# A Macaron block with an SSM and FP4 layers on one core: one projection for B, C and dt, other engines for part of the layernorm, and a new order with tables of its own at the ends

## The chip, the core and the metric

The kernel runs on one core of a Trainium2 chip. The metric is the device time of one execution in microseconds (us); the figure given for a kernel is the median of its runs. The engines are PE (TensorE), DVE (VectorE), ACT (ScalarE), POOL (GpSimd) and SP (SyncE, which issues the transfers). Each works through its own instructions in the order in which they were written; semaphores order them across engines.

## What is computed

The input `x` is 32 batches of 512 rows by 256 columns, in float32. Each batch goes through three layers, each with a layernorm in front and a residual sum behind:

```python
x = x + 0.5 * ffn(layernorm(x))      # "ffn 0"
x = x + ssm(layernorm(x))            # "ssm"
x = x + 0.5 * ffn(layernorm(x))      # "ffn 1"

def ffn(x):                          # w_gate, w_up: 704 x 256, w_down: 256 x 704
    xq = fp4(x)                      # per 16 values: scale = max|x| / 6, round to the FP4 grid
    h = silu(xq @ fp4(w_gate).T) * (xq @ fp4(w_up).T)
    return fp4(h) @ fp4(w_down).T

def ssm(x):                          # 16 states per column
    Bm, Cm = split(x @ W_in + b_in)  # 16 + 16 columns
    dt = clip(softplus((x @ W_dt1 + b_dt1) @ W_dt2 + b_dt2), 1e-7, 1e6)
    a = exp(A * dt)
    b = expm1(A * dt) / (A * dt) * dt * Bm * x
    h[l] = a[l] * h[l - 1] + b[l]    # a scan over the 512 rows, for each column and state
    return sum(h * Cm, states) + D * x
```

## The kernel before

**Layout.** A batch of 512 rows lies in SBUF as four tiles of 128 rows (`x0` to `x3`, one per stage). The FFN works per row tile: `gate` and `up` (L676), `silu` and `up copy` on ACT, `product` on POOL (L699, for the first tile of ffn 0 on DVE, L692), then the quantizing of the hidden 704 columns, six transposes (L710), and `down` (L722) with the residual (L726); `sum` (L729) copies the result from PSUM. The SSM works on transposed data, columns on partitions, 512 rows along the free axis: `bc` and `dt1` are two products with `xT` (L741), each with a bias step on ACT (L745, L752); `dt2` (L757), softplus (L761) in place in PSUM, and a clip on DVE (L764) give `dt`. B and C go through DRAM (`rows`) and come back broadcast to all partitions (L780, L782). For each half of the columns and each pair of states: exp and tanh on ACT (L789, L792), `x b` on POOL (L796), `e`, `e x b` and the scan on DVE (L803, L806, L809), `h c` on POOL (L812), and PE adds the states up in PSUM (L818). expm1 is made from tanh, since expm1(t) = (exp(t) + 1) tanh(t / 2).

**Layernorm** (L502). For each of four row tiles DVE computes bn_stats and their aggregation; POOL makes the reciprocal root and the shift of all four in four instructions on four columns each (L512 to L519); ACT applies them (`normal`, L522).

**Quantizing** (L527). DVE takes the maximum of each block, scales, inverts and makes the quotient (L544 to L550). The maximum and the reciprocal lie in PSUM. ACT squares the quotient and applies a line to it (`square` L554, `curve` L556, both to bfloat16); PE adds that number to the quotient in PSUM and takes it away again (`grid`, L563), whereby the quotient is rounded to the grid; ACT copies it out (`rounded`, L569) and POOL multiplies it by the scale (`value`, L570).

**Order.** Nothing is scheduled by the framework. `Plan` gets every step with the buffers it reads and writes. Each has a time from the table `WHEN`, plus `PERIOD` (3379) times the number of its batch; `Plan.run` takes the steps by that time, each as soon as all that it depends on has been taken and its buffers are free, and writes them out in that order. So the steps of several batches interleave on each engine, and the same order repeats from batch to batch. The weights are quantized in the same plan, at the start.

Of the kernel before, what the change touches and what calls it, by code (L numbers as in the profile page):

```python
# [16 lines left out]
P = 128  # L17
# [13 lines left out]
WHEN = {  # L31
        "weights load": (7249, 7248, 7249, 7249, 6726, 6726, 6642, 6642, 6642, 6841, 6841, 6841,
        6841),
        "weights x top": (7249, 7065, 7353),
        "weights x scale": (7250, 7248, 7385),
        "weights x rinv": (7250, 7248, 7391),
        "weights x quotient": (7250, 7248, 7391),
        "weights x square": (7250, 7249, 7392),
        "weights x curve": (7250, 7249, 7392),
        "weights x grid": (7250, 7249, 7557),  # L40
        "weights x rounded": (7250, 7249, 7557),
        "weights x value": (7250, 7249, 7558),
        "weights turn": (7251, 7251, 7249, 7249, 7558, 7558),
        "weights turned": (7251, 7251, 7250, 7251, 7558, 7558),
        "weights load down": (7065, 6579),
        "weights h top": (7558, 6642),
        "weights h scale": (7571, 6642),
        "weights h rinv": (7571, 6642),
        "weights h quotient": (7571, 6643),
        "weights h square": (7590, 6643),  # L50
        "weights h curve": (7590, 6643),
        "weights h grid": (7590, 6643),
        "weights h rounded": (7590, 6643),
        "weights h value": (7795, 7065),
        "weights turn down": (7795, 7795, 7699, 7661),
        "weights turned down": (7897, 7814, 8179, 7699),
        "weights zero rows": (8077, 8345),
        "in load": (0,),
        "ffn 0 stats": (1267, 1773, 601, 2361),
        "ffn 0 mean": (1913, 2355, 1536, 3584),  # L60
        "ffn 0 var + eps": (4038,),
        "ffn 0 rstd": (4045,),
        "ffn 0 - mean": (3609,),
        "ffn 0 shift": (4249,),
        "ffn 0 normal": (4499, 5056, 6579, 4467),
        "ffn 0 x top": (6643,),
        "ffn 0 x scale": (6726,),
        "ffn 0 x rinv": (6822,),
        "ffn 0 x quotient": (6835,),
        "ffn 0 x square": (6841,),  # L70
        "ffn 0 x curve": (6873,),
        "ffn 0 x grid": (6880,),
        "ffn 0 x rounded": (6950,),
        "ffn 0 x value": (6969,),
        "ffn 0 xqT turn": (7065, 7129),
        "ffn 0 xqT turned": (7136, 7168),
        "ffn 0 tile 0 gate": (7353, 7251),
        "ffn 0 tile 0 silu": (7437, 7321),
        "ffn 0 tile 0 up": (7577, 7558),
        "ffn 0 tile 0 up silu": (7584, 7571),  # L80
        "ffn 0 tile 0 h top": (7590,),
        "ffn 0 tile 0 h scale": (7609,),
        "ffn 0 tile 0 h rinv": (7661,),
        "ffn 0 tile 0 h quotient": (7705,),
        "ffn 0 tile 0 h square": (7737,),
        "ffn 0 tile 0 h curve": (7808,),
        "ffn 0 tile 0 h grid": (7814,),
        "ffn 0 tile 0 h rounded": (7897,),
        "ffn 0 tile 0 h value": (8045,),
        "ffn 0 tile 0 turn h": (8301, 8192),  # L90
        "ffn 0 tile 0 turned h": (8352, 8339),
        "ffn 0 tile 0 down": (8397,),
        "ffn 0 tile 0 sum": (8461,),
        "ffn 0 tile 1 gate": (7385, 7392),
        "ffn 0 tile 1 silu": (7449, 7507),
        "ffn 0 tile 1 up": (7622, 7667),
        "ffn 0 tile 1 up copy": (7718, 7699),
        "ffn 0 tile 1 product": (7795,),
        "ffn 0 tile 1 h top": (7923,),
        "ffn 0 tile 1 h scale": (8000,),  # L100
        "ffn 0 tile 1 h rinv": (8032,),
        "ffn 0 tile 1 h quotient": (8121,),
        "ffn 0 tile 1 h square": (8179,),
        "ffn 0 tile 1 h curve": (8205,),
        "ffn 0 tile 1 h grid": (8217,),
        "ffn 0 tile 1 h rounded": (8275,),
        "ffn 0 tile 1 h value": (8416,),
        "ffn 0 tile 1 turn h": (8493, 8441),
        "ffn 0 tile 1 turned h": (8544, 8512),
        "ffn 0 tile 1 down": (8563,),  # L110
        "ffn 0 tile 1 sum": (8781,),
        "ffn 0 tile 2 gate": (8083, 8064),
        "ffn 0 tile 2 silu": (8096, 8070),
        "ffn 0 tile 2 up": (8134, 8345),
        "ffn 0 tile 2 up copy": (8256, 8390),
        "ffn 0 tile 2 product": (8429,),
        "ffn 0 tile 2 h top": (8576,),
        "ffn 0 tile 2 h scale": (8653,),
        "ffn 0 tile 2 h rinv": (8704,),
        "ffn 0 tile 2 h quotient": (8729,),  # L120
        "ffn 0 tile 2 h square": (8813,),
        "ffn 0 tile 2 h curve": (8838,),
        "ffn 0 tile 2 h grid": (8857,),
        "ffn 0 tile 2 h rounded": (8953,),
        "ffn 0 tile 2 h value": (8979,),
        "ffn 0 tile 2 turn h": (9088, 9081),
        "ffn 0 tile 2 turned h": (9165, 9126),
        "ffn 0 tile 2 down": (9222,),
        "ffn 0 tile 2 sum": (9267,),
        "ffn 0 tile 3 gate": (8077, 8109),  # L130
        "ffn 0 tile 3 silu": (8089, 8211),
        "ffn 0 tile 3 up": (8928, 8985),
        "ffn 0 tile 3 up copy": (9069, 9094),
        "ffn 0 tile 3 product": (9101,),
        "ffn 0 tile 3 h top": (9357,),
        "ffn 0 tile 3 h scale": (9376,),
        "ffn 0 tile 3 h rinv": (9440,),
        "ffn 0 tile 3 h quotient": (9472,),
        "ffn 0 tile 3 h square": (9510,),
        "ffn 0 tile 3 h curve": (9529,),  # L140
        "ffn 0 tile 3 h grid": (9587,),
        "ffn 0 tile 3 h rounded": (9613,),
        "ffn 0 tile 3 h value": (9677,),
        "ffn 0 tile 3 turn h": (9837, 9843),
        "ffn 0 tile 3 turned h": (9869, 9856),
        "ffn 0 tile 3 down": (9920,),
        "ffn 0 tile 3 sum": (9984,),
        "ssm stats": (8768, 8992, 9517, 10048),
        "ssm mean": (9325, 9369, 9933, 10093),
        "ssm var + eps": (10099,),  # L150
        "ssm rstd": (10150,),
        "ssm - mean": (10157,),
        "ssm shift": (10163,),
        "ssm normal": (10182, 10169, 10227, 10176),
        "ssm xT turn": (10233, 10246),
        "ssm xT turned": (10304, 10310),
        "ssm bc": (10425,),
        "ssm bc bias": (10489,),
        "ssm rows": (10656,),
        "ssm dt1": (10317,),  # L160
        "ssm dt1 bias": (10451,),
        "ssm dt2": (10464, 10521),
        "ssm softplus": (10598, 10617),
        "ssm dt": (10681, 10688),
        "ssm skip": (11481, 13229),
        "ssm load b": (10720, 10790, 10854, 11270, 11232, 11712, 11648, 11917, 12115, 12294,
        12563, 12723, 13005, 13139, 13318, 13792),
        "ssm load c": (10809, 11161, 11328, 11846, 11641, 11974, 12153, 12345, 12627, 12825,
        13190, 13101, 13568, 13945, 14029, 14041),
        "ssm exp": (10925, 11021, 11059, 11014, 11289, 11341, 11347, 11027, 11750, 11993, 12038,  # L170
        12000, 12006, 11961, 12422, 12352, 12582, 12179, 12569, 12813, 12934, 12941, 13088, 13113,
        13376, 13120, 13382, 13305, 13753, 13849, 13504, 13811),
        "ssm tanh": (10976, 11033, 11110, 11283, 11334, 11494, 11737, 11693, 11878, 11987, 12077,
        12102, 12281, 12262, 12486, 12403, 12614, 12710, 12845, 12774, 13043, 13069, 13273, 13254,
        13491, 13408, 13670, 13734, 13837, 13907, 14093, 14125),
        "ssm x b": (10726, 11155, 11206, 11661, 11616, 12064, 11897, 12288, 12537, 12633, 12883,
        13017, 13209, 13574, 13657, 13971),
        "ssm e": (10982, 11104, 11129, 11296, 11507, 11520, 11763, 11699, 11885, 12025, 12134,
        12141, 12377, 12339, 12512, 12435, 12678, 12742, 12915, 12857, 13049, 13081, 13344, 13261,
        13587, 13523, 13715, 13773, 13920, 13933, 14163, 14214),  # L180
        "ssm e x b": (10995, 11136, 11213, 11373, 11577, 11603, 11827, 11801, 11936, 12057, 12243,
# [99 lines left out]
        "ffn 1 tile 3 down": (18112,),  # L281
        "ffn 1 tile 3 sum": (18157,),
        "out store": (19712,),
}


class Buf:
# [599 lines left out]
```

## Time and profile before

| | before |
|---|---|
| median of 3 runs | 3604.15 us (3602.44 to 3604.26) |
| the profiled execution | 3604.13 us |
| its span, first to last instruction | 3602.2 us |
| granted TensorE clock, mean | 0.984 |
| busy: PE, DVE, ACT, POOL | 3348.0, 3409.9, 3385.7, 3332.3 us |
| idle DVE time between 480 and 3360 us | 17.8 us of 2880 |
| ACT table loads | 284, 1283 ns each |

A group of instructions is one line of the profile: the line of the kernel, the engine, the operation, the tile written and the tiles read (buffer numbers left out), the shapes and the count; then the busy time of the group in us and the mean of one instruction in ns; then the time in which the engine sat idle just before them, and whose end it waited for. TensorE runs a float32 product as two matmul records. A wait is told as the engine and the line that waited, what ended the wait, the sum in us, how many there were, and the longest. A line of the table by stages names the stretch and its length, then each engine's busy time and number of instructions, then the granted TensorE clock, the busy share of the DMA engines, and GB/s. In the list of instructions by time each line has the start, the duration, and how many equal ones it merges.

### The profile page before, as it was taken

The page shows a single profiled execution, that of the slowest core. Times are in us where ns is not written, and L with a number is a line of the kernel's source. Part 1 is how long each engine was busy: PE and PEld are TensorE (multiplying, and loading weights), DVE is VectorE, ACT ScalarE, POOL GpSimd, SP SyncE. Part 2 cuts the span into 40 slices and gives each one's busy share as a digit, 9 for nine tenths or more (in the row PEclk, how much of TensorE's full clock was granted, in tenths as well). Part 3 has the DMA queues.
Part 4 walks back from the last instruction along what each step waited for, and adds up shares of the span by engine and source line. Part 5 has one row for each costly group of instructions (what it writes and reads, how often), then busy time and mean ns, then how long its engine had stood idle before and what let it go on. Part 6 is the DMA issues. An engine that isn't in the chain of part 4 may idle for free. (4 is left out here: it accounts for less than half of the span.)

```text
span 3602.2 us, 51333 instructions
## 1 busy us (share of the span) xinstructions
PE 3348.0 (93%) x16604; PEld 2443.6 (68%) x16826; DVE 3409.9 (95%) x5280; ACT 3385.7 (94%) x5813; POOL 3332.3 (93%) x1963
## 2 busy tenths in 40 slices
PE   5779999999999999999999999999999999999966
PEld 3457777667767767777766776776777776777654
DVE  3699999999999999999999999999999999999992
ACT  4689999999999999999999999999999999999973
POOL 2589999999999999999999999999999999999992
PEclk9899999999999999999999999999999999999988
DMA  1354545444545545454544454444555454445440
GB/s 45 112 173 166 173 164 176 165 169 165 176 171 170 165 158 175 170 173 164 177 165 169 165 176 170 170 165 159 176 171 173 163 177 165 168 161 169 171 170 12
DMA packets 186652, 578.36 MB, mean 161 GB/s; under 512 B 19664, under 2 KB 54032, under 8 KB 186384
## 3 DMA queue, kind: packets, MB, share of 16 engines
q1 hardware_dynamic: 184816, 574.89, 46.7%
q8 instruction: 133, 2.18, 0.2%
q14 instruction: 135, 1.11, 0.1%
q10 hardware_dynamic: 1568, 0.18, 0.0%
HBM read 556.12 MB, written 18.87 MB: 160 GB/s over the span
## 5 line engine op out<-in xcount | busy, mean ns | idle before, releaser
L676 PE MATMUL pt<-w_guT,xqT 128*128 128x352 f32 x4096 | 1317.4, 466 | 26.1 <-DVE dt L764 16.3
L812 POOL TENSOR_TENSOR hs<-hs,bc 128x1024 f32<-128x1024 f32 x512 | 1214.0, 2371 | 9.3 <-DVE hs L809 2.6
L809 DVE TENSOR_TENSOR_SCAN hs<-ab,eb 128x512 f32<-128x512 f32 x1024 | 1202.4, 1197 | 4.5
L796 POOL TENSOR_TENSOR bx<-xT,bc 128x1024 f32<-128x1024 f32 x512 | 1171.2, 2294 | 30.3 <-DVE eb L806 15.9
L676 PEld LDWEIGHTS pt<-w_guT,xqT 128*128 128x128 f32 x4096 | 753.3, 192 | 409.7 <-DVE dt L764 24.0
L792 ACT ACTIVATE eb<-dt,a_half 128x512 f32<-128x512 f32 x1024 | 708.1, 700 | 36.1 <-DVE hs L809 29.5
L806 DVE SCALAR_TENSOR_TENSOR eb<-eb,a_inv,bx 128x512 f32<-128x512 f32 x1024 | 734.9, 743 | 2.7
L722 PE MATMUL pt<-w_dT,hqT 128*128 128x256 f32 x3072 | 717.0, 383 | 14.8 <-ACT hqT L715 14.8
L789 ACT ACTIVATE ab<-dt,a_sb 128x512 f32<-128x512 f32 x1024 | 700.8, 727 | 1.5
L803 DVE SCALAR_TENSOR_TENSOR eb<-ab,eb 128x512 f32<-128x512 f32 x1024 | 684.5, 682 | 11.4 <-ACT eb L792 7.6
L722 PEld LDWEIGHTS pt<-w_dT,hqT 128*128 128x128 f32 x3072 | 580.1, 192 | 140.4 <-ACT hqT L715 32.9
L818 PE MATMUL py<-ident,hs 128*128 128x128 f32 x4096 | 536.1, 276 | 26.1 <-POOL hs L812 25.8
L818 PEld LDWEIGHTS py<-ident,hs 128*128 128x128 f32 x4096 | 469.4, 142 | 102.0 <-POOL hs L812 38.3
L570 POOL TENSOR_TENSOR h_q<-h_q,h_sc 128x704 f32<-128x704 f32 x258 | 360.3, 1397 | 53.2 <-ACT h_q L569 52.6
L699 POOL TENSOR_TENSOR h<-h,sl 128x704 f32<-128x704 f32 x224 | 379.0, 1692 | 27.4 <-ACT h L696 22.4
L544 DVE TENSOR_REDUCE q<-h 128x44 f32<-128x704 f32 x258 | 227.0, 880 | 68.6 <-POOL h L699 43.8
L710 PE MATMUL pt<-ident,h_q 128*128 128x128 f32 x1536 | 237.0, 278 | 41.2 <-ACT h L696 24.1
L563 PE MATMUL q<-h_m,eye 128*128 128x192 bf16 (+1 forms) x873 | 191.6, 305 | 70.9 <-ACT h_m L556 62.0
L710 PEld LDWEIGHTS pt<-ident,h_q 128*128 128x128 f32 x1536 | 180.5, 141 | 110.3 <-ACT h L696 51.8
L563 PEld LDWEIGHTS <-eye 128*128 128x128 bf16 x1300 | 125.2, 99 | 183.9 <-issue 106.8
L715 ACT COPY hqT<-pt 128x256 f32<-128x256 f32 (+1 forms) x512 | 233.9, 487 | 6.1 <-PE pt L710 5.7
L686 ACT ACTIVATE sl<-pt 128x352 f32<-128x352 f32 x512 | 222.5, 463 | 16.6 <-PE pt L676 13.8
(78 smaller groups left out, 4134.6 us busy)
## 6 DMA issues: line engine op xcount, KB each, us to landing
bc<-rows SPq DMA_DIRECT2D x1024, 512.0 KB, 4.1
x<-in_L_attn_x_dram SPq DMA_DIRECT2D x32, 512.0 KB, 5.2
out_dram<-x SPq DMA_DIRECT2D x32, 512.0 KB, 7.3
rows<-bc SPq DMA_DIRECT2D x32, 64.0 KB, 3.4
xn<-in_L_ffn_w_up_dram SPq DMA_DIRECT2D x6, 128.0 KB, 2.2
h<-in_L_ffn_w_down_dram SPq DMA_DIRECT2D x2, 352.0 KB, 3.4
xn<-in_L_ffn_w_gate_dram SPq DMA_DIRECT2D x5, 128.0 KB, 2.2
w_dt_sb<-in_L_attn_W_dt_dram ACTq DMA_DIRECT2D x2, 64.0 KB, 5.5
```

Of the source, the lines that this page charges most:

```text
L676: pe.matmul(to()[:, :HALF], lhsT=xqT()[:, c, j * P : (j + 1) * P], rhs=w_guT()[:, c, o : o + HALF], start=(c == 0), stop=(c == NC - 1),)
L699: op("POOL", "product", lambda sl=sl, h=h: g.tensor_tensor(h(), h(), sl(), ALU.mult), [h, sl], [h])
L710: pe.transpose(pt()[:, i * P : (i + 1) * P], hq()[:, kcol[k] : kcol[k] + P], ident)
L722: pe.matmul(po()[:, :DM], lhsT=hqT()[:, k, :], rhs=w_dT()[:, k, :], start=(k == 0), stop=False,)
L789: op("ACT", "exp", lambda c=c, i=i, k=k, ab=ab: s.activation(ab()[:, i, :], dt()[:, c, :], AF.Exp, scale=a_sb[:, c, k : k + 1]), [(dt, c)] ...
L792: op("ACT", "tanh", lambda c=c, i=i, k=k, eb=eb: s.activation(eb[i](), dt()[:, c, :], AF.Tanh, scale=a_half[:, c, k : k + 1]), [(dt, c)], ...
L796: op("POOL", "x b", lambda c=c, bx=bx, bn=bn: g.tensor_tensor(bx().rearrange("p n l -> p l n"), xT()[:, c, :].unsqueeze(2).to_broadcast([P ...
L803: op("DVE", "e", lambda i=i, ab=ab, eb=eb: v.scalar_tensor_tensor(eb[i](), ab()[:, i, :], 1.0, eb[i](), ALU.add, ALU.mult), [(ab, i), eb[i ...
L806: op("DVE", "e x b", lambda c=c, i=i, k=n + i, eb=eb, bx=bx: v.scalar_tensor_tensor(eb[i](), eb[i](), a_inv[:, c, k : k + 1], bx()[:, i, : ...
L809: op("DVE", "scan", lambda i=i, h=h, ab=ab, eb=eb: v.tensor_tensor_scan(h()[:, i, :], ab()[:, i, :], eb[i](), 0.0, ALU.mult, ALU.add), [(a ...
L812: op("POOL", "h c", lambda h=h, cn=cn: g.tensor_tensor(flat(h()), flat(h()), flat(cn()), ALU.mult), [h, cn], [h])
L818: pe.matmul(py()[:, j, :], lhsT=h()[:, i, j * P : (j + 1) * P], rhs=ident, is_transpose=True, start=False, stop=False, skip_group_check=True,)
```

## The change

- `bc` and `dt1` become one product with 96 output rows and one bias step (`project`): dt1's 64 rows first, B's and C's 32 behind.
- The layernorm of the SSM gets its sums from ACT: `sum` of ffn 0 also gives the sum of each row, DVE makes the negative mean of it (`mean`), and ACT squares the difference and sums that (`spread`, four). POOL applies the layernorm (`normal`, four).
- In all three layernorms, var + eps and the shift are one DVE instruction each; POOL keeps the power (`rstd`).
- The `curve` of three hidden tiles (ffn 0 tiles 1 and 3, ffn 1 tile 3) goes from ACT to DVE, on the bfloat16 tile in SBUF. For tile 2 of ffn 1, one DVE instruction makes `value` from PSUM, in place of `rounded` on ACT and `value` on POOL.
- Softplus writes `dt` to SBUF, and POOL clips it there.
- `WHEN` has new times for all steps; batches 0, 1, the last but one and the last have tables of their own (`FIRST`, `SECOND`, `LAST_BUT_ONE`, `LAST`). `PERIOD` stays.

With the options as they are set, `x b` is the same instruction as before. In the diff the tables and the parts that follow from the names are cut.

```diff
 PERIOD = 3379
-WHEN = {
...
+WHEN = {
...
+FIRST = {
+    **WHEN,
...
+PRODUCT_BY_DVE = {(0, 0)}
+VALUE_BY_DVE = {(1, 2)}
+CURVE_BY_DVE = {(1, 3), (0, 1), (0, 3)}
+NORMAL_BY = {"ffn 0": "ACT", "ssm": "POOL", "ffn 1": "ACT"}
+STATS_BY = {"ffn 0": "DVE", "ssm": "sum", "ffn 1": "DVE"}
+CLIP_BY = "POOL"
+XB_INNER = True
...
-        o.at = (WHEN[o.name][k] + self.batch * PERIOD, len(self.ops))
+        table = self.tables.get(self.batch, WHEN)
+        o.at = (table[o.name][k] + self.batch * PERIOD, len(self.ops))
...
-    plan = Plan()
+    plan = Plan({0: FIRST, 1: SECOND, NB - 2: LAST_BUT_ONE, NB - 1: LAST})
...
-        op("POOL", "var + eps", lambda: g.tensor_tensor(
-            rstd(), mv()[:, :, 1], eps, ALU.add), [mv], [rstd])
+            op("DVE", "var + eps", lambda: v.tensor_scalar(
+                rstd(), mv()[:, :, 1], LN_EPS, None, ALU.add), [mv], [rstd])
+            mean, sign = (lambda: mv()[:, :, 0]), -1.0
+            means = mv
+        else:
...
+            op("DVE", "mean", lambda: v.tensor_scalar(
+                means(), sums(), -1.0 / DM, None, ALU.mult), [sums], [means])
+            for j in range(NJ):
+                op("ACT", "spread", lambda j=j: s.activation(
+                    dst()[:, on(j)], src()[:, j, :], AF.Square, bias=means()[:, j : j + 1],
+                    accum_out=square()[:, j : j + 1]),
+                   [(src, j), means], [(dst, j), (square, j)])
+            op("DVE", "var + eps", lambda: v.tensor_scalar(
+                rstd(), square(), 1.0 / DM, LN_EPS, ALU.mult, ALU.add), [square], [rstd])
+            mean, sign = (lambda: means()), 1.0
         op("POOL", "rstd", lambda: g.tensor_tensor(rstd(), rstd(), neg_half, ALU.pow),
            [rstd], [rstd])
-        op("POOL", "- mean", lambda: g.tensor_tensor(
-            shift(), mv()[:, :, 0], minus_one, ALU.mult), [mv], [shift])
-        op("POOL", "shift", lambda: g.tensor_tensor(shift(), shift(), rstd(), ALU.mult),
-           [shift, rstd], [shift])
+        op("DVE", "shift", lambda: v.scalar_tensor_tensor(
+            shift(), mean(), sign, rstd(), ALU.mult, ALU.mult), [means, rstd], [shift])
...
+                op("POOL", "normal", lambda j=j: g.tensor_scalar(
+                    dst()[:, on(j)], src()[:, j, :], rstd()[:, j : j + 1],
+                    shift()[:, j : j + 1], ALU.mult, ALU.add),
+                   [(src, j), rstd, shift], [(dst, j)])
...
+        if what in CURVE_BY_DVE:
+            op("DVE", f"{tag} curve", lambda: v.tensor_scalar(
+                c(), c(), CURVE / 6.0, CURVE * 4.0 / 3.0, ALU.mult, ALU.add), [c], [c])
...
+        if what in VALUE_BY_DVE:
+            op("DVE", f"{tag} value", lambda: v.tensor_tensor(
+                blocks(dst()), blocks(q()[:, :F]), spread(scale()), ALU.mult),
+               [(q, "q"), scale], [dst])
+            return dst
...
+                op("ACT", "sum", lambda j=j, po=po: s.activation(
+                    dst()[:, j, :], po()[:, :DM], AF.Copy, accum_out=sums()[:, j : j + 1]),
+                   [po], [(dst, j), (sums, j)])
...
+                pe.matmul(pbc()[: R + 2 * N, :], lhsT=w_p_sb[:, c, :], rhs=xT()[:, c, :],
+                          start=(c == 0), stop=(c == NC - 1))
...
+                op("ACT", "softplus", lambda c=c: s.activation(
+                    dt()[:, c, :], p2[c](), AF.Softplus, bias=b_dt2_sb[:, c : c + 1]),
+                   p2[c:], [(dt, c)])
+                op("POOL", "dt", lambda c=c: g.tensor_scalar(
+                    dt()[:, c, :], dt()[:, c, :], 1e6, 1e-7, ALU.min, ALU.max),
+                   [(dt, c)], [(dt, c)])
```

## The prediction

> **What bounds the kernel now.** I read the page's header and engine totals first, then the table by stages, the waits of VectorE (DVE), and last the groups that the change touches.
>
> ```profile
> span 3602.2 us, 51333 instructions
> PE 3348.0 (93%) x16604; PEld 2443.6 (68%) x16826; DVE 3409.9 (95%) x5280; ACT 3385.7 (94%) x5813; POOL 3332.3 (93%) x1963
> ```
>
> Four engines within 2.3% of each other. The table by stages tells which is first (columns: PE, PEld, DVE, ACT, POOL):
>
> ```profile
> 0.00:60.00 60.00, 24.91 (x74) 13.85 (x76) 22.78 (x51) 26.15 (x35) 12.82 (x19) 0.97 0.23 68
> 60.00:120.00 60.00, 44.94 (x174) 29.26 (x175) 17.41 (x39) 29.04 (x54) 15.54 (x14) 0.86 0.03 9
> 480.00:3360.00 2880.00, 2781.51 (x13993) 2040.10 (x14183) 2862.16 (x4428) 2840.98 (x4899) 2809.51 (x1647) 1.00 0.50 169
> 3480.00:3540.00 60.00, 36.26 (x184) 27.50 (x186) 42.01 (x62) 33.40 (x57) 38.65 (x23) 0.84 0.25 86
> ```
>
> Between 480 and 3360 us DVE is busy 99.4%, ACT 98.6%, POOL 97.6%, PE 96.6%. The scan (L809) runs 866 times there, 32 to a batch: 27.06 batches, so 106.4 us per batch; 32 of them are 3405 us, and the remaining 197 us of the span are the two ends. Per batch DVE works 105.8 us, ACT 105.0, POOL 103.8, PE 102.8. In that stretch DVE's whole list of waits is this:
>
> ```profile
> DVE eb L803 <- ACT eb L792: 0.6, 2, 0.5
> DVE h L692 <- PE pt L676: 0.6, 2, 0.3
> DVE q L544 <- ACT x_q L569: 0.5, 2, 0.3
> ```
>
> DVE sets the period: a microsecond per batch on DVE is a microsecond of time, elsewhere nothing until that engine passes it. Of the groups, these carry the sums:
>
> ```profile
> L570 POOL TENSOR_TENSOR h_q<-h_q,h_sc 128x704 f32<-128x704 f32 x258 | 360.3, 1397 | 53.2 <-ACT h_q L569 52.6 <-DVE eb L806 0.4
> L550 DVE SCALAR_TENSOR_TENSOR q<-h,q 128x704 f32<-128x704 f32 x258 | 226.7, 879 | 1.4
> L556 ACT ACTIVATE h_m<-h_m 128x704 bf16<-128x704 bf16 x258 | 205.4, 796 | 2.6
> L509 DVE BATCH_NORM_AGGREGATE mv<-stats 128x2 f32<-128x6 f32 x384 | 61.7, 168 | 0.1
> ```
>
> Neighbours overlap: DVE's groups add up to 3742.4 us against 3409.9 busy, 63 ns per instruction; the same reckoning gives 70 ns on ACT and 40 on POOL. I charge each instruction its mean less that.
>
> **The change, per batch.** *DVE* loses four bn_stats (417 ns) and four aggregations (168) of the SSM layernorm and two clips of dt (671): 4×0.354 + 4×0.105 + 2×0.608 = 3.05 us. It gains one value step on 704 columns from PSUM; its nearest row is the quotient L550: 0.82. It gains seven instructions on four columns (one mean, three var + eps, three shifts); nearest the aggregation: 7×0.105 = 0.74. It gains three curves on 704 bf16 columns, SBUF to SBUF. That form stands only at the start, once each:
>
> ```profile
> 7.60 0.18 DVE L476 TENSOR_SCALAR a_half<-a_sb 128x32 f32<-128x32 f32 x1 [1.86 <-DMA a_sb<-in_L_attn_A_dram]
> 10.98 0.22 DVE L489 TENSOR_SCALAR eye<-ident 128x128 bf16<-128x128 f32 x1
> ```
>
> By the unrounded 181 and 220 ns, 96 more columns cost 39 ns, 0.41 per column; L550 against its 1024-column form (1217) gives 1.06. A curve is then 168 + 704×0.41 = 457 ns; half the slope (two-byte data) 312, the slow slope 914. Three: 1.18 us (0.75 to 2.55). Net on DVE: 0.82 + 0.74 + 1.18 − 3.05 = −0.3 us (−0.7 to +1.1), if nothing holds these instructions up.
>
> *What may hold them up.* In steady work every DVE instruction of before reads one tensor from SBUF at most, the other from PSUM (top, reciprocal, `eb`, softplus), and none is a one-source tensor_scalar from SBUF to SBUF; all durations there lie close (the quotient 868 to 897 ns). The change puts in ten per batch of other forms: three curves, three var + eps and the mean are SBUF-to-SBUF tensor_scalars; each shift reads two SBUF tensors. The 0.41 ns per column says that the first kind streams more than one column per DVE step, so it uses more of SBUF than the rest. No row shows it beside working POOL: L476 and L489 ran while POOL was idle; `diag_d` (L481, 271 and 282 ns) met at most one four-column POOL instruction and shows no wait, weak evidence for freedom. Bounds per instruction: nothing, and a whole POOL instruction, 2.37 us (L812). Between them I take the rest of the POOL instruction in progress. A batch's POOL work is 16×2.371, 16×2.290, 7×1.692, 8×1.397, 2×1.936, 3×1.007; a random busy moment falls in an instruction of (sum of squares)/(sum) = 2.12 us, half of which is left. With POOL 91% busy in a longer period that is 0.96 us, ten times 9.6 us. I choose it over nothing because the ten use SBUF as no steady row does. Behind a blocked one stand the e, e x b and scan of the states in its queue, and `h c` on POOL, the tanh that needs an `eb` and the state sums on PE wait for those.
>
> [...]
>
> *POOL* loses nine small layernorm steps (0.16 each) and one value (1.36), 2.82 us; `rstd` stays. It gains four normals (256 columns) and two clips (512). From L570 (704 to 1024 columns, 1397 to 1936 ns) a column is 1.68 ns plus 0.21: 0.64 and 1.07 us, 4×0.60 + 2×1.03 = 4.46. Net +1.6: 105.4. At the two-tensor slope (2.12 ns, L699 to L812) +2.5; at the ident select's (128 columns in 292 ns) −0.4.
>
> [...]
>
> *ACT* loses four normals (590), three curves (796), a rounded (756) and one of two bias steps (about 0.68): 4×0.52 + 3×0.73 + 0.69 + 0.61 = 5.6 us. It gains four squares on 256 columns at the normal's price and eight accumulated sums that no row shows: between nothing and a whole 256-column copy less overlap (0.30). Taking 0.15: 4×0.52 + 8×0.15 = 3.3. Net −2.3 (−3.5 to −1.1), down to 102.7. The table loads stay (284 before, 285 after). *PE* drops half of L741 (62.1 + 60.9 us): −1.9, down to 100.9. Neither sets the period, so their savings bring nothing.
>
> *Order and ends.* The layernorm chain of the SSM gets longer: mean (DVE), squares (ACT), var + eps (DVE), power (POOL), shift (DVE), normals on POOL, behind two 2.3 us products in the steady order, then PE's turns behind them; the clips too move into POOL's queue ahead of the exp on ACT. In the table a batch runs from 6643 (first quantize) to 18157 (last sum), 3.4 periods of 3379, so over three batches overlap, which hides this. SP issues the same transfers in a new order; DMA is at 0.50, and its landings cost POOL 5.9 us in the stretch. At the ends, the new order has 104 DVE instructions ahead of the first scan (101 before), 239 PE ones ahead of the first dt2 (237), and 33 on DVE after the last scan (29): the same shape. I charge zero, bounds ±25 us.
>
> **Sum.** −0.3 + 9.6 = +9.3 us per batch. DVE is full from 360 to 3420 us, 28.8 batches; elsewhere its idle time absorbs the waits. 28.8×9.3 = 268, on the span of 3602.2: 3870. The profiled run took 3604.13, 1.9 outside the span, which stands at the median of 3604.15: about 3872, say 3870. With waits of 0.5 to 1.3 us each: 3739 to 3969.
>
> **Rivals.** *A: no blocking, faster.* The mechanism is DVE's lighter sum: −0.3 gives 10 us in 32 batches, −0.7 gives 22, good ends up to 25 more: 3555 to 3597, most likely 3585. For it: the steady DVE rows never stretch, and `diag_d` beside POOL. It decides when the ten waits together stay under 0.3 us a batch, 30 ns each. *B: no blocking, but a new bound.* POOL at 106.3 us with today's 0.6 us of idle gives 106.9, +0.5×32 = +16; curves on the slow slope give +1.1×32 = +35: 3611 to 3660. *C: gains and costs meet,* 3597 to 3611: what the change frees lies on ACT and PE, which are not the bound, so it may do nothing.
>
> **Chances.** Blocking 0.58, A 0.27, B 0.12, C 0.03. A measurement here tells some 0.2%, 7 us, from no change: faster 0.27, same 0.03, slower 0.70. The range leaves out the better half of A and the top of the blocking case: 3570 to 3930; the likeliest case alone 3739 to 3969.
>
> **What would show it.** Right: four-column DVE instructions (var + eps, shift, mean) of about 1 us where the aggregation has 0.17, curves of 1.2 to 1.5, DVE still 99% busy, POOL, ACT and PE near 91, 89 and 87%, a period near 115.7. Wrong: those rows at 0.1 to 0.2 us; then the period is near 106, and either DVE still waits for nothing (A) or POOL fills up (B). A DVE list of waits headed by POOL's power or ACT's squares would mean that the longer chain is not hidden, which I have at nothing.

## The result, and the profile after

The changed kernel takes 3868.41 us (median; 3863.73 to 3871.03) against 3603.72 us beside it: a ratio of 1.0734, with an interval of 1.0715 to 1.0752. That the forecast of 3870 was met to 2 us is luck: its main assumption, that POOL's instructions hold up DVE's new ones, held, but its terms were off by more than that, and their errors cancel. The profiled execution took 3863.73 us.

The page's header and engine totals:

```profile
span 3861.9 us, 51137 instructions
PE 3371.9 (87%) x16698; PEld 2449.1 (63%) x16698; DVE 3643.8 (94%) x5310; ACT 3343.3 (87%) x5910; POOL 3359.5 (87%) x1835
```

The table by stages (columns: PE, PEld, DVE, ACT, POOL; granted clock, DMA share, GB/s). The last line lies about as far from the end as its counterpart of before (120 and 122 us):

```profile
0.00:60.00 60.00, 30.12 (x107) 17.79 (x108) 27.98 (x63) 30.35 (x43) 12.21 (x13) 0.91 0.23 68
60.00:120.00 60.00, 47.74 (x185) 31.45 (x183) 17.85 (x38) 36.77 (x73) 23.44 (x19) 0.89 0.18 59
480.00:3360.00 2880.00, 2592.03 (x12994) 1889.44 (x12994) 2823.25 (x4120) 2592.05 (x4598) 2614.66 (x1425) 0.99 0.46 156
3741.80:3801.80 60.00, 42.43 (x221) 34.44 (x219) 46.92 (x70) 33.41 (x59) 44.00 (x22) 0.85 0.37 123
```

DVE is still nearly full from 480 to 3360 us (98.0%); the others fell to 90.0, 90.0 and 90.8%. The scan runs 800 times there: 25.0 batches, 115.2 us each, where it was 106.4. Per batch DVE is busy 112.9 us (105.8 before) and idle 2.3 (0.7). So of the 8.8 us that a batch grew, 7.2 are DVE's busy time, which counts the hold-ups inside its instructions, and 1.6 are idle time. The ends did not matter much: the span less 32 periods is 176 us, against 197.

DVE's waits in that stretch:

```profile
DVE eb L1741 <- ACT eb L1733: 25.9, 46, 1.5
DVE q L1458 <- ACT h_q L1492: 7.6, 25, 0.3
DVE h_m L1471 <- ACT h_m L1468: 5.5, 24, 0.2
DVE eb L1741 <- ACT ab L1730: 1.4, 9, 0.2
```

The first is an exp that comes late, 1.0 us per batch; before, the whole list came to 1.7 us in 27 batches. The groups of the steps that changed, and of two that did not:

```profile
L1464 DVE SCALAR_TENSOR_TENSOR q<-h,q 128x704 f32<-128x704 f32 x258 | 227.4, 881 | 0.8
L1488 DVE TENSOR_TENSOR h_q<-q,h_sc 128x704 f32<-128x704 f32 x32 | 27.9, 872 | 2.7 <-PE q L1481 2.6
L1400 DVE BATCH_NORM_AGGREGATE mv<-stats 128x2 f32<-128x6 f32 x256 | 40.9, 173 | 0.1
L1471 DVE TENSOR_SCALAR h_m<-h_m 128x704 bf16<-128x704 bf16 x96 | 159.7, 1663 | 10.2 <-ACT h_m L1468 10.2
L1427 DVE SCALAR_TENSOR_TENSOR shift<-mv,rstd 128x4 f32<-128x4 f32 x64 | 57.0, 890 | 2.2 <-POOL rstd L1425 2.2
L1427 DVE SCALAR_TENSOR_TENSOR shift<-means,rstd 128x4 f32<-128x4 f32 x32 | 39.9, 1245 | 1.1 <-POOL rstd L1425 1.1
L1415 DVE TENSOR_SCALAR means<-sums 128x4 f32<-128x4 f32 x32 | 21.7, 677 | 10.0 <-ACT x L1656 10.0
L1402 DVE TENSOR_SCALAR rstd<-mv 128x4 f32<-128x4 f32 x64 | 15.5, 243 | 0.2
L1422 DVE TENSOR_SCALAR rstd<-square 128x4 f32<-128x4 f32 x32 | 7.7, 240 | 0.3 <-ACT xn_s L1418 0.3
```

The quotient (L1464) and the aggregation (L1400) cost what they did. So does the new value step (L1488), which reads one tensor from PSUM: 872 ns, predicted at 879. A shift of four columns, however, takes as long as a value step of 704. Most of that time is not work, and none of it counts as idle: the idle figure of each row stands behind the second bar, and the wait sits inside the duration itself. A list of one line's instructions (durations: shortest, median, longest) shows that no such row has one price:

```profile
L1471 DVE TENSOR_SCALAR h_m<-h_m x74: 408/1959/3281, 526.3 to 3339.3; 128x704 bf16<-128x704 bf16 x74
L1427 DVE SCALAR_TENSOR_TENSOR shift<-mv,rstd x50: 176/835/2307, 479.8 to 3347.2; 128x4 f32<-128x4 f32 x50
```

What they wait for is seen when DVE and POOL are laid side by side. DVE by time (start, duration):

```profile
2024.88 2.13 DVE L1471 TENSOR_SCALAR h_m<-h_m 128x704 bf16<-128x704 bf16 x1
2026.93 1.40 DVE L1744 SCALAR_TENSOR_TENSOR eb<-eb,a_inv,bx 128x512 f32<-128x512 f32 x2
```

and POOL in the same time:

```profile
2024.45 2.36 POOL L1750 TENSOR_TENSOR hs<-hs,bc 128x1024 f32<-128x1024 f32 x1
2026.77 1.78 POOL L1622 TENSOR_TENSOR h<-h,sl 128x704 f32<-128x704 f32 x1
```

The curve began 0.43 us into POOL's `h c` and ended 0.20 us after it (2027.01 against 2026.81). POOL's next instruction took 1.78 us where its group has a mean of 1.69. Taking all rows between 480 and 3360 us: all 74 curves end 194 to 206 ns after the end of a POOL instruction, and all 74 shifts and all 25 means 11 to 30 ns after one. Of the 75 var + eps none ends within 60 ns of one (they take 135 to 165 ns and are free), nor does any of the 200 hidden quotients and 199 aggregations. Even the shortest curve of the stretch (408 ns) has a hold-up in it: at the two ends of the run, where no POOL instruction was in progress when they began, five curves took 333 to 344 ns.

### The profile page after: what moved, and what is told of

Same layout as the page of the kernel before. It is cut to its first block, busy times and chain, and to the rows that moved or that the text cites. A ratio compares the mean times of both kernels' runs of the same rounds, so it can differ in the third digit from the quotient of the medians.

```text
span 3861.9 us, 51137 instructions
## 1 busy us (share of the span) xinstructions
PE 3371.9 (87%) x16698; PEld 2449.1 (63%) x16698; DVE 3643.8 (94%) x5310; ACT 3343.3 (87%) x5910; POOL 3359.5 (87%) x1835
## 4 chain that ended last, share of the span: by engine, by line
DVE 41%; ACT 25%; PE 22%; issue 5%; POOL 1%; DMA 0%; DVEq 0%; ACTq 0%; POOLq 0%; SPq 0%
DVE hs L1747 12%; PE pt L1599 9%; DVE eb L1741 7%; DVE eb L1744 7%; PE pt L1645 5%; ACT eb L1733 4%; ACT ab L1730 4%; DVE h_m L1471 3%; DVE q L1464 3%; DVE q L1458 3%; PE q L1481 3%; ACT h_m L1468 2%; PE py L1756 2%; ACT h_q L1492 2%; ACT h_m L1474 2%
## 5 line engine op out<-in xcount | busy, mean ns | idle before, releaser
L1599 PE MATMUL pt<-w_guT,xqT 128*128 128x352 f32 x4096 | 1332.8, 469 | 17.4 <-ACT sl L1609 10.6
L1599 PEld LDWEIGHTS pt<-w_guT,xqT 128*128 128x128 f32 x4096 | 744.6, 192 | 422.7 <-ACT sl L1609 47.3
L1744 DVE SCALAR_TENSOR_TENSOR eb<-eb,a_inv,bx 128x512 f32<-128x512 f32 x1024 | 749.0, 748 | 17.6 <-POOL bx L1701 1.4
L1756 PEld LDWEIGHTS py<-ident,hs 128*128 128x128 f32 x4096 | 480.9, 145 | 99.6 <-POOL hs L1750 63.7
L1493 POOL TENSOR_TENSOR h_q<-h_q,h_sc 128x704 f32<-128x704 f32 x226 | 314.2, 1390 | 68.0 <-ACT h_q L1492 66.1
L1481 PE MATMUL q<-h_m,eye 128*128 128x512 bf16 (+1 forms) x1032 | 206.3, 324 | 176.0 <-DVE h_m L1471 132.0
L1638 ACT COPY hqT<-pt 128x512 f32<-128x512 f32 (+1 forms) x512 | 239.5, 477 | 51.2 <-PE pt L1633 49.3
```

Source lines behind the costliest of these rows:

```text
L1481: pe.matmul(q()[:, cols], lhsT=eye, rhs=c()[:, cols], start=False, stop=eye is minus, skip_group_check=True,)
L1599: pe.matmul(to()[:, :HALF], lhsT=xqT()[:, c, j * P : (j + 1) * P], rhs=w_guT()[:, c, o : o + HALF], start=(c == 0), stop=(c == NC - 1),)
L1744: op("DVE", "e x b", lambda c=c, i=i, k=n + i, eb=eb, bx=bx: v.scalar_tensor_tensor(eb[i](), eb[i](), a_inv[:, c, k : k + 1], bx()[:, i, : ...
L1756: pe.matmul(py()[:, j, :], lhsT=h()[:, i, j * P : (j + 1) * P], rhs=ident, is_transpose=True, start=False, stop=False, skip_group_check=True,)
```

## The experiments

A period below is 32 times 2880 us divided by the number of scans between 480 and 3360 us, as in the prediction. Times are medians; each ratio is to the kernel before. Where an expectation speaks of a port that DVE and POOL share, that is the author's assumption: the traces show that a DVE instruction is held and with which POOL instruction it ends, and no run shows a port.

### Taking the suspected instructions off DVE

`curve_act`: the three curves go back to ACT.

```diff
-CURVE_BY_DVE = {(1, 3), (0, 1), (0, 3)}
+CURVE_BY_DVE = set()
```

> The three curves of each batch go back from DVE to ACT; all else, the times in the tables too, is as in the changed kernel. Port theory (a DVE instruction that needs the port shared with POOL waits for the POOL instruction in progress): DVE loses 3 x (1.66 - 0.06) = 4.8 us per batch, of which 3.6 was waiting; ACT gains 2.2 and stays below DVE; 4.8 x 29.5 batches = 142 us, so about 3726 us, and the shifts still show 0.9 to 1.3 us each. Order theory (the new tables and the longer layernorm chain cost the time, the long rows are only where it shows): the time stays within 40 us of 3868, and DVE waits elsewhere instead.

Measured: 3776.38 us, 1.0481 (1.0466 to 1.0497), period 112.3. The shifts still take 792 and 1262 ns. The gain is 92 us, halfway between the two expectations. DVE's waits:

```profile
DVE eb L1741 <- ACT eb L1733: 35.9, 93, 1.2
DVE q L1458 <- ACT h_q L1492: 33.5, 74, 0.9
DVE pt L1458 <- ACT hqT L1638: 17.7, 24, 1.4
```

DVE's idle time per batch rose from 2.3 to 4.4 us, most of it spent waiting for ACT, which has three curves more: part of what the blocked curves cost turned into a new wait.

`minis_pool`: the seven four-column steps go to POOL, the curves stay on DVE.

```diff
-            op("DVE", "var + eps", lambda: v.tensor_scalar(
+            op("POOL", "var + eps", lambda: g.tensor_scalar(
...
-            op("DVE", "mean", lambda: v.tensor_scalar(
+            op("POOL", "mean", lambda: g.tensor_scalar(
...
-        op("DVE", "shift", lambda: v.scalar_tensor_tensor(
-            shift(), mean(), sign, rstd(), ALU.mult, ALU.mult), [means, rstd], [shift])
+        def shifted():
+            g.tensor_tensor(shift(), mean(), rstd(), ALU.mult)
+            if sign < 0:
+                g.tensor_scalar(shift(), shift(), -1.0, None, ALU.mult)
```

> Mean, var + eps and shift of all three layernorms go from DVE to POOL (nine or ten instructions on four columns per batch there); the curves stay on DVE. Port theory: DVE loses (21.7 + 15.5 + 7.7 + 57.0 + 39.9) / 32 = 4.4 us per batch less 0.4 of overlap, 4.0; POOL gains about 1.6 and stays below DVE; 4.0 x 29.5 = 118 us, so about 3750 us, and the curves still show about 1.7 us each. Order theory: within 40 us of 3868.

Measured: 3741.97 us, 1.0381 (1.0366 to 1.0397), period 110.5. The time is as expected, but not for the reason expected, since the curves, which were to stay at 1.7 us, became shorter as well:

```profile
L1475 DVE TENSOR_SCALAR h_m<-h_m 128x704 bf16<-128x704 bf16 x96 | 101.9, 1061 | 28.6 <-ACT h_m L1472 28.6
```

Between 480 and 3360 us, DVE's rows lose 4.3 us per batch with the four-column steps and 2.4 with the curves, which still end with POOL's instructions, but begin at other moments of them (median 449 ns, where it was 1959). So the 126 us are not the price of the four-column steps alone; these were to be less than one microsecond per batch (seven times 0.105).

`both`: the two edits together; none of the ten is left on DVE.

> [...] Port theory: DVE falls to 112.9 - 8.8 = 104.1 us per batch; POOL at about 106.2 and ACT at about 105.9 become the bound; 32 x 107 + 176 at the ends = 3600 us, within 30, so no slower than the kernel before. Order theory: it stays above 3750 us, since tables, chain, squares with sums, POOL's normals and clips are all still there.

Measured: 3709.96 us, 1.0292 (1.0277 to 1.0308), period 109.5: a clear miss of the first expectation, and below the second. 158 of the 265 us come back, the rest stays although none of the ten steps is on DVE any more. Stage table:

```profile
480.00:3360.00 2880.00, 2688.19 (x13658) 1960.15 (x13657) 2758.89 (x4065) 2763.05 (x4915) 2798.32 (x1732) 1.00 0.48 164
```

Over 26.3 batches DVE works 104.9 us and idles 4.6, mostly for ACT (41 of the 121 us in the stretch for its exp, 30 for `rounded`, 20 for the turned hidden tile); POOL works 106.3 of 109.5 us. The engine that was to be relieved no longer sets the period.

### Keeping the work on DVE in a form that does not wait

`forms`: the curve reads its tile as 11 rows of 64 that lie 66 apart; the shift is four instructions on one column, with `rstd` as a per-partition scalar; the mean is on ACT.

```diff
+            cp = new(pool, [P, 11, 66], BF16, "h_mp", 2)
...
-                c(), c(), CURVE / 6.0, CURVE * 4.0 / 3.0, ALU.mult, ALU.add), [c], [c])
+                c(), cp()[:, :, :64], CURVE / 6.0, CURVE * 4.0 / 3.0, ALU.mult, ALU.add),
+               [cp], [c])
...
-            shift(), mean(), sign, rstd(), ALU.mult, ALU.mult), [means, rstd], [shift])
+            for j in range(NJ):
+                v.tensor_scalar(shift()[:, j : j + 1], mean()[:, j : j + 1], rstd()[:, j : j + 1],
+                                sign, ALU.mult, ALU.mult)
```

> [...] Port theory: curves fall from 1.66 to 0.5 to 0.9 us each, shifts to 0.1 to 0.2 for each of the four, none ends with a POOL instruction; DVE at about 107 us per batch, 32 x 108 + 176 = 3630 us, within 40. If instead the instructions were slow in themselves (bfloat16, four columns, a late semaphore), curves stay at 1.5 us or more and the time above 3750 us.

Measured: 3689.02 us, 1.023 (1.0213 to 1.0248), period 108.9. Groups:

```profile
L1476 DVE TENSOR_SCALAR h_m<-h_mp 128x704 bf16<-128x704 bf16 x96 | 49.3, 514 | 9.8 <-ACT h_mp L1473 9.7
L1428 DVE TENSOR_SCALAR shift<-mv,rstd 128x1 f32<-128x1 f32 x256 | 36.2, 205 | 2.2 <-POOL rstd L1424 2.2
L1421 DVE TENSOR_SCALAR rstd<-square 128x4 f32<-128x4 f32 x32 | 16.6, 518 | 9.7 <-ACT xn_s L1417 9.7
```

The same curve takes 514 ns instead of 1663 on the same engine beside POOL's work, and its ends no longer follow POOL's: none of the 79 between 480 and 3360 us ends within 280 ns after one. For the shift the run does not tell whether the operands or the length decided, since both changed. The var + eps of the SSM, which was free in that stretch, now takes 518 ns and ends 24 to 30 ns after a POOL instruction (25 of 26): whether an instruction waits depends on where it falls. DVE still has 107.0 us of work and 1.9 of idle time, and the time is above the range expected.

`forms_pool`: as `forms`, but the shift goes to POOL as in `minis_pool`, which leaves var + eps as the only ones of the ten steps that still wait.

> [...] Twelve one-column shifts at 0.14 us less on DVE than in the run with forms alone: DVE falls from 107.0 to 105.3 us per batch, POOL rises from 104.3 to 105.1. If DVE's work is all that is left over: period 109.2 - 1.7 = 107.5, about 3635 us. If the changed kernel loses the rest to waits of its order (layernorm chain, tables made for other durations): between 3660 and 3710 us, with DVE idle 3 us or more per batch.

Measured: 3663.8 us, 1.0167 (1.0152 to 1.0183), period 108.0. Stage table:

```profile
480.00:3360.00 2880.00, 2706.93 (x13817) 1984.41 (x13816) 2823.31 (x4268) 2746.54 (x4927) 2803.66 (x1648) 1.00 0.48 166
```

DVE's work is 105.9 us per batch, that of before, but the period is 1.6 us above the old one: DVE idles 2.1 us, and POOL is busy 97.3%. The time lies in the range of the second expectation, but the idle time of 3 us or more that it named did not appear. The var + eps now wait too (353 and 437 ns on average in the stretch, where the changed kernel has 154 and 161), 0.7 us per batch. It is the fastest version of the changed kernel, and still 60 us slower than before.

### The three curves alone, in the kernel before

`b_curve` puts the three curves on DVE in the old kernel, with no other edit; `b_rows` does the same in the padded form.

```diff
-        op("ACT", f"{tag} curve", lambda: s.activation(
-            c(), c(), AF.Identity, bias=CURVE * 4.0 / 3.0, scale=CURVE / 6.0), [c], [c])
+        if what in CURVE_BY_DVE:
+            op("DVE", f"{tag} curve", lambda: v.tensor_scalar(
+                c(), c(), CURVE / 6.0, CURVE * 4.0 / 3.0, ALU.mult, ALU.add), [c], [c])
+        else:
...
```

> The kernel before with one part of the change alone: the three curves go from ACT to DVE as the change has them, SBUF to SBUF in place; tables and all else as before. Port theory: 1.66 us each as in the changed kernel, so DVE gains 3 x 1.6 = 4.8 us per batch, 138 us over 28.8 batches: about 3743 us (3690 to 3790, since the rest of the POOL instruction that each meets depends on the order). If the new order were needed for the loss: about 3604 + 40.

> [...] Port theory: 0.51 us each as measured in this form, 3 x 0.45 = 1.35 us per batch, 39 to 43 us: about 3645 us; the difference to the run with the plain form, about 100 us, is the waits alone, with the same engines and the same order. If DVE's curve cost more for another reason (a hop between engines more, PE's wait for it): as slow as the plain form.

Measured: `b_curve` 3823.1 us, 1.0607 (1.0589 to 1.0624), period 113.5; `b_rows` 3639.28 us, 1.0095 (1.008 to 1.011), period 107.5. The curve of `b_curve`:

```profile
L559 DVE TENSOR_SCALAR h_m<-h_m 128x704 bf16<-128x704 bf16 x96 | 231.5, 2411 | 4.5 <-ACT h_m L556 2.1
```

and of `b_rows`:

```profile
L561 DVE TENSOR_SCALAR h_m<-h_mp 128x704 bf16<-128x704 bf16 x96 | 49.3, 514 | 4.6 <-ACT h_mp L558 2.1
```

The two kernels differ in the layout of one tile and by 184 us. The rows give the same: (2411 − 514) × 96 = 182 us. DVE's idle time is the same in both (0.6 us per batch), and no other DVE row differs by more than 0.12 us per batch, so the difference is the collision, shown; bfloat16 or the extra hop between engines, which both kernels have, is not the cause. It is more than was expected for `b_curve`, because a static order does not make the start of the wait random: 70 of 76 curves in the stretch end 195 to 268 ns after a POOL instruction and take 2.0 to 3.7 us, most of one instruction each time and for 23 of them the next one as well. The other six met none and took 337 to 341 ns. `b_rows` came out as expected: 3 × (514 − 63) ns on a full DVE is 1.35 us a batch, 43 us in 32 batches (36 measured), and the three curves ACT is rid of bring nothing.

### The other parts of the change, in the kernel before

`b_value`: the one projection, the clip on POOL and the value step on DVE, with the due time that the value has in the old table, 17369.

```diff
         "ffn 1 tile 2 h value": (17369,),
...
+    VALUE_BY_DVE = {(1, 2)}
...
+        op("PE", "project", project, [xT], [pbc])
...
-            op("DVE", "dt", lambda c=c: v.tensor_scalar(
-                dt()[:, c, :], p2[c](), 1e-7, 1e6, ALU.max, ALU.min), [p2[c]], [(dt, c)])
+            op("POOL", "dt", lambda c=c: g.tensor_scalar(
+                dt()[:, c, :], dt()[:, c, :], 1e6, 1e-7, ALU.min, ALU.max), [(dt, c)], [(dt, c)])
```

> [...] DVE: 0.81 - 1.22 = -0.4 us per batch, ACT -1.3, POOL 1.15 - 1.36 = -0.2, PE -1.9. Port theory: nothing waits, 0.4 x 32 = 13 us saved: about 3591 us, faster than both kernels. Rival: POOL and ACT, 97 to 98% busy, are as good as full and the clip behind POOL's products makes the exps late: 3604 to 3625 us.

Measured: 3644.74 us, 1.0111 (1.0096 to 1.0126), above both expectations. The miss has a place, the first of DVE's waits:

```profile
DVE h_q L568 <- PE q L561: 47.0, 27, 3.3
```

1.7 us per batch: the value stood too early in DVE's queue and held up all behind it. `b_value_late` and `b_value_later` move it back, to 17450 and 17500, and change nothing else.

> The kernel before with one projection, the value of one tile on DVE from PSUM and the clip on POOL, as tried (3645 us), but that value 81 units later in the table: it then stands behind two e x b and two scans in DVE's queue (3.7 us more work) and no longer waits 1.7 us per batch for PE's grid. If that wait was the loss: 1.7 x 32 = 55 us less, about 3590 us, faster than both kernels. If ACT and POOL are in truth full (clips, later exps), it stays above 3620 us and DVE waits elsewhere.

> The same with the value 131 units later, behind one bn_stats more. If the wait for the grid still had a rest at 81 units: some us faster than that one; if not, equal within 5 us, about 3590 us.

Measured: 3598.0 us (3595.3 to 3600.29), 0.9982 (0.9974 to 0.9991), and 3599.25 us, 0.9983 (0.9974 to 0.9992). The wait is gone; the longest left in DVE's list is this one of `b_value_late`:

```profile
DVE eb L802 <- ACT eb L791: 0.6, 2, 0.5
```

These two beat both kernels, by 6 and 5 us, at the edge of what can be told from no change. The work taken off DVE, 2 × 0.61 − 0.81 = 0.4 us a batch, would be 13 us; about half of it came in the whole time. In the steady stretch nearly all of it did (869 scans where there were 866: a period of 106.05, 0.37 us less).

`b_clip`: as these, with the one projection, but without the value step: POOL only takes on the clips, DVE only loses them.

> The kernel before with one projection and the clip of dt on POOL, and nothing on DVE in return (all values on POOL): DVE 105.8 - 1.2 = 104.6 us per batch, ACT 104.4, POOL 105.0, PE 100.9. If the order leaves the bound engine 0.6 us idle as today, POOL sets 105.6 us: 0.8 x 32 = 26 us less, about 3578 us. If POOL can't be filled beyond the 97.6% that it has (its gaps between instructions count too), the period is 107.6 us: about 3640 us, slower than the kernel before.

Measured: 3635.78 us, 1.0089 (1.0076 to 1.0103): 1.1 us a batch less on the engine that bounds the kernel (104.7 against 105.8), and 32 us more. Stage table:

```profile
480.00:3360.00 2880.00, 2708.43 (x13747) 2006.94 (x13934) 2806.79 (x4326) 2803.35 (x4821) 2813.81 (x1684) 1.00 0.50 167
```

POOL is as full as before (97.7%), DVE is not (97.5%). The heads of two lists: DVE now waits for PE's `up`, and PE waits for POOL's `h c`:

```profile
DVE h L695 <- PE pt L679: 53.5, 53, 1.3
```

```profile
PE py L817 <- POOL hs L811: 39.8, 54, 1.3
```

Before, the two came to 0.6 and 6.2 us. POOL was not filled further: the 1.1 us a batch put on it (104.9 against 103.8) came out as 1.0 us of period, as the second expectation had it.

### The tables of the ends

`forms_mid`: `forms` with the table for batch 0 alone.

```diff
-    plan = Plan({0: FIRST, 1: SECOND, NB - 2: LAST_BUT_ONE, NB - 1: LAST})
+    plan = Plan({0: FIRST})
```

> [...] If the tables at the ends save time: 3700 to 3715 us. If they do nothing, as the equal numbers of instructions ahead of the first scan and behind the last one let me think: 3689 within 8.

Measured: 3746.56 us, 1.0389 (1.0374 to 1.0405), above both expectations, at nearly the period of `forms` (109.2 and 108.9). The 193rd scan starts at 841.0 us against 783.6 in `forms`, and the last scan stands 83.7 us before the end against 74.1. So the tables are worth 58 us here, nearly all at the start; but FIRST was made to go with SECOND, so this is the price of half a set, not the gain over the old ends. Between before and after the ends shrank: 85.8 against 73.6 us from the last scan to the end, 135.9 against 122.1 us to the first. How much of that the tables did, and how much the rest of the change, no run separates.

## Why the prediction was right, and where not

**DVE as the bound.** Right for the kernel before, and shown by `b_rows`: 1.2 us of work per batch added to DVE came out as 1.1 us of period, and work taken from ACT brought nothing. The converse, that work taken off DVE is time gained, was seen only where POOL did not get it instead: `b_value_late`, with 0.4 us less on DVE and 0.2 less on POOL, gained 0.4 us a batch; `b_clip`, with 1.1 less on DVE and 1.1 more on POOL, lost 1.0. POOL has an idle time of its own, 2.6 us per batch before, where rival B gave it DVE's 0.6. With 2.6 us, POOL's work gives 107.5 for `b_clip` (104.9; measured 107.4), 107.8 for `forms_pool` (105.2; measured 108.0) and 108.9 for `both` (106.3; measured 109.5). That POOL's load is what holds these three up is argued from this agreement and from `b_clip`, not shown. Half of POOL's idle time, before and in `b_clip`, is one wait in the order, for the statistics of a layernorm:

```profile
POOL rstd L512 <- DVE mv L509: 35.4, 54, 1.0
```

```profile
POOL rstd L508 <- DVE mv L505: 36.0, 53, 1.0
```

In `forms_pool` and `both` POOL's idle time lies elsewhere, in `forms_pool` first in waits for B and C from DRAM (18.2 us). No run moved these steps, so whether POOL could be filled further is open.

**The waits.** That POOL holds up DVE is right; the size was off. Seven of the ten steps wait, not ten: the var + eps have nothing to meet, since POOL stands waiting for them (its `rstd` idles 92.5 us behind them). Less a free one (the shortest curve, 408 ns, the shortest shift, 176, and for the mean the aggregation's 173), the means of the stretch are 1.42 us for a curve, 0.88 for a shift, 0.44 for the mean: 3 × 1.42 + 3 × 0.88 + 0.44 = 7.3 us per batch, where the sum had ten times 0.96. (By the free ones at the ends, 333 to 344 ns for a curve and from 135 for a shift, it is some 0.3 us more.) The term that failed is the random moment: the order fixes where in a POOL instruction each step falls (the shifts of the SSM take 1306 to 1362 ns, all 25 of them), so the mean rest of an instruction is no more than a guess for each row. (The 2.12 us in the prediction should read 2.11, which leaves the 0.96 as it is.)

That a step is held until POOL's instruction ends was an assumption: no run or row of before shows it, nor the term of ten times 0.96 us that was worked out from it. In the changed kernel the ends show it, 11 to 30 ns after POOL's for four columns and 194 to 206 for a curve, and in place of the 9.6 us stand the 7.3. Nor does any run show that the ten use more of SBUF than other rows: the two slopes in the prediction, 0.41 and 1.06 ns per column, are times alone, and a curve of 704 columns that met no POOL instruction took 333 to 344 ns. What frees the padded curve, its 11 rows or the gaps between them, the runs do not separate; its 514 ns and its ends apart from POOL's are what was measured.

**DVE's own work.** −0.3 us was right within 0.2: 7.3 − 0.3 is 7.0, and DVE's busy time rose by 7.2. The curve without a wait was put at 457 ns and takes 333 to 344 where POOL does not hold it; the value step at 879 and is 872.

**The order.** Charged at nothing, it cost 1.6 us per batch of DVE's time, chiefly in waits for ACT's exp (1.0 us). That the exp is late because of the blocked steps is not shown: in `both`, where none is left, DVE waits for it longer (41 us against 26). This miss and the smaller waits cancel: 7.2 + 1.6 = 8.8 against 9.3, and so the period is 115.2 against 115.7. Two more cancel in the time: the sum charged 28.8 batches, where 8.8 us in all 32 are 281 us, and the ends gave back 21. What the prediction named as the sign of an unhidden chain (waits for POOL's power or ACT's squares) did not appear.

**The other engines.** POOL was put at 105.4 and is 104.6 us: a clip takes 613 ns (put at 1.07 us) and a normal 558 (0.64). ACT, put at 102.7, is 103.7. Each accumulated sum is an instruction of its own with a median of 187 or 196 ns, near the middle of the bounds, so the miss does not lie there: ACT's rows add up to 3.4 us less per batch, its busy time to 1.3 less, as its neighbours overlap less than before. PE is 103.7, not 100.9; in part its rows are longer at a clock of 0.99 (gate and up 469 ns, before 466), and the rest is open. None of this touches the bound in this kernel.

**The ends.** Zero with ±25 us held: the ends shrank by 21.

**The rivals.** A fell with its premise, and the runs without most of the waits speak against it too: `both` and `forms_pool` are slower than before by 105 and 60 us. That is where B's range of 3611 to 3660 ends and beyond it (3663.8 and 3709.96). Of the loss of 265 us, some 205 hang on the form and the place of seven DVE instructions per batch (the changed kernel against `forms_pool`: three curves, four-column shifts and the mean); the remaining 60 I put down to the fuller POOL, the waits of var + eps that are left and the order, together and unseparated.

## What to carry to other kernels

Before a small step moves to VectorE, look at what it reads and writes and at what GpSimd is doing then: a step of four columns took up to 2.3 us here (the longest shift, 2307 ns), and the profile shows none of the hold-up as idle. If a row's durations spread widely, compare the ends of its instructions with those of the other engine; a change of layout may be all that is needed (514 ns in `b_rows` where `b_curve` has 2411). And an engine at 97% may be as good as full in a given order: in `b_clip`, 1.1 us more on such an engine cost 1.0 us of period, though the engine at 99% was relieved. Look first at what it waits for in its remaining time.

## What was not expected of the hardware

A curve can wait for two POOL instructions one after the other: the longest took 3281 ns here, and 3.7 us in `b_curve`. A four-column step ends 11 to 30 ns after the POOL instruction that holds it, a curve 194 to 206 ns after, over half of the 333 to 344 that it takes when free. The same 704 columns read as 11 rows of 64, 66 apart, take 514 ns in `forms`, where none of the 79 ends within 280 ns after a POOL instruction; a one-column shift with a per-partition scalar takes 200 to 205 ns on average there, where four columns took 890 and 1245. The wait also works the other way, if little: the 20 products of POOL that had begun when a curve ended took 1771 to 1795 ns, the other 204 took 1659 to 1745. In `b_curve` the same holds for POOL's `rstd <- mv` on four columns: 292 to 392 ns for 22 of them, 191 to 209 for the other 74.
